# A graph network's first layer: low nodes' counts stored by themselves, dense part begun earlier, fewer edges ahead of it

## The chip, the core and the metric

The kernel runs on one core of a Trainium2 chip. The core has a matrix engine (PE, with its weight loads shown as PEld), a vector engine (DVE), a scalar engine (ACT), a general engine (POOL) and a sequencer that issues most of the transfers (SP). Each engine works through its own instructions in order; engines wait for one another with semaphores. The metric is the device time of one execution in microseconds, smaller is better.

## What is computed

The reference runs four blocks one after the other on 3125 nodes with 256 features and 100000 edges sorted by target node: a two-layer graph attention network, a dense mixture of experts, a two-layer graph convolution, and a routed mixture of experts. The change concerns the first attention layer only:

```python
def gat_conv(x, src, dst, W, a_src, a_dst, bias, concat):
    h = (x @ W).reshape(N, H, C)              # H = 4 heads, C = 256
    al_s = jnp.einsum('nhc,hc->nh', h, a_src)
    al_d = jnp.einsum('nhc,hc->nh', h, a_dst)
    e = jax.nn.leaky_relu(al_s[src] + al_d[dst], 0.2)
    ex = jnp.exp(e - m[dst])                  # m: maximum over the edges of a target
    denom = jax.ops.segment_sum(ex, dst, num_segments=N)
    alpha = ex / denom[dst]
    out = jax.ops.segment_sum(h[src] * alpha[:, :, None], dst, num_segments=N)
```

Each node also has an edge to itself. Targets are drawn so that low node numbers have by far the most edges.

## The kernel before

The class `FirstLayer` does three things in one loop.

*Counts.* The edges are cut into 391 chunks of 256. For each chunk (`count_step`) DVE makes one-hot matrices of the sources' high part (`hot_key`, line 1649) and of their low part (`hot_lo`, on DVE at line 1652 or in three passes on ACT at lines 1655 and 1658), PE multiplies them (line 1666), and the result, a window of 8, 14 or 20 target nodes, goes into an accumulator `acc` of 320 targets: ACT copies all columns but the first (`keep`, line 1683), DVE adds the first (`add`, line 1688). The place in `acc` is a register's value. When all chunks of 320 targets are done (`CUT`, for the first at chunk 128), `piece` opens the next accumulator, `add_own` adds the nodes' own edges and `store_counts` writes 320 columns to DRAM in five transfers. Behind the first of them `low_degrees` (25 matmuls, line 1712) sums the counts of nodes 0 to 255. The later layers need all counts.

*Dense part.* For targets 0 to 255 (`DN`) the layer is computed with dense matrices: the loop reads their counts back from DRAM (`lead`, line 1990), makes the weights on ACT (lines 2003 and 2005) and DVE (line 2010), and PE multiplies them by all source rows (line 2019): 4 heads by 25 blocks of sources, 100 dense steps (`dense_step`).

*Edge part.* For targets from 256 up, 283 chunks of edges are summed one by one (`edge_step`). POOL gathers the source rows, two gathers a chunk, 12 chunks ahead (line 1773); small transfers on SP fetch the targets' terms (`window`, lines 1783 and 1786) two batches of four chunks ahead; PE picks the terms (line 1807) and multiplies (lines 1839 and 1845); DVE adds the result into a sum `agg` of 384 targets (line 1856). For each of the 8 sets of 384 targets, `new_sums` lists tasks: `clear`, then three times `loops` (the nodes' own edges: line 1909 multiplies `x` with the weights `by_node`, which are read back from the DRAM tensor `loops`, spread over all partitions; a transpose and a copy at lines 1914 and 1915 put the weights themselves into the sum), then `done`. `first_terms` writes `loops` at line 1595, one row of 4 numbers per node. Finished sums go through `through_w1` (14 tasks).

The loop in `run` fixes the order by hand. Before it 26 chunks of counts are made, the sums of set 0 are prepared with `new_sums(0)` (a chunk of counts behind each task), and the first batch of edges is prepared. In the loop each step makes one chunk of counts, at most one task from a queue, the edge steps that `share` calls for, and the dense steps that are due. `lead(0)` comes at step `d0` (134), the first dense step four steps later. Up to `d1` = `d0` + 3 the edge steps are spread so that `FIRST` = 45 are done by then; the remaining ones are spread evenly up to the last chunk. After each step PE, DVE and ACT are tied to that order (`in_order`).

## Time and profile before

| | us |
|---|---|
| median of 9 runs | 2705.96 |
| lowest and highest | 2696.09, 2712.39 |
| the profiled execution | 2706.09 |
| its span | 2704.2 |
| first chunk of counts (line 1649) starts | 62.1 |
| last chunk of counts starts | 1119.7 |
| last statistics of the first layer's output (line 1976) | 1164.8 |
| PE, DVE, ACT, POOL busy, share of the span | 87%, 51%, 42%, 30% |

The span begins with the program's first instruction and ends with its last. A line of the profile with a count, such as x782, tells how many instructions it sums; "idle before" is the time for which the engine had nothing to do ahead of them, with what ended it. Matmuls are pipelined, so that the durations of single ones overlap.

### The profile page before, as it was taken

What the parts mean: (1) busy time and instruction counts of PE and PEld (TensorE: products, weight loads), DVE (VectorE), ACT (ScalarE), POOL (GpSimd) and SP (SyncE); (2) the same over time, 40 slices, a digit from 0 to 9 for tenths busy, and PEclk for the clock granted to TensorE, in tenths of its full rate; (3) what the DMA queues carried; (4) which work ended last, traced back from release to release, by engine and by line L of the source; (5) the groups of instructions that cost most, each with busy time, mean ns of one, the idle gap of its engine ahead of it and who ended that gap; (6) DMA issues with size and microseconds to landing.
All of it is one profiled execution on the core that took longest, in us unless ns stands there. A gap on an engine that the chain in (4) does not pass through costs nothing. (4 is left out here: it accounts for less than half of the span.)

```text
span 2704.2 us, 38772 instructions
## 1 busy us (share of the span) xinstructions
PE 2347.1 (87%) x11821; PEld 1905.9 (70%) x11821; DVE 1387.5 (51%) x4378; ACT 1143.5 (42%) x2527; POOL 823.2 (30%) x803
## 2 busy tenths in 40 slices
PE   1488998888888889677999979988989998999997
PEld 1367786766666666466888858877867766888886
DVE  7566546566666677621888844242334664111110
ACT  0256544545555555350444434444433433222221
POOL 1265556656666677120010030000001123122221
PEclk9999868778879888888999979999999998999998
DMA  6543435454554565489512110004324425666662
GB/s 194 83 117 85 116 102 174 112 158 124 167 146 141 168 179 172 122 291 312 171 62 73 62 47 1 1 1 135 121 86 143 135 96 181 190 175 174 190 182 61
DMA packets 242046, 355.01 MB, mean 131 GB/s; under 512 B 45680, under 2 KB 183251, under 8 KB 238114
## 3 DMA queue, kind: packets, MB, share of 16 engines
q1 hardware_dynamic: 198082, 253.10, 30.1%
q0 software_dynamic: 40176, 94.81, 13.9%
q10 hardware_dynamic: 3568, 4.47, 0.5%
q8 instruction: 100, 1.64, 0.3%
q14 instruction: 120, 0.98, 0.1%
HBM read 266.60 MB, written 86.86 MB: 131 GB/s over the span
## 5 line engine op out<-in xcount | busy, mean ns | idle before, releaser
L1773 POOL DMA_INDIRECT edge_rows<-table,pick x566 | 599.3, 1059 | 364.2 <-PE edge_sums L1839 176.7
L1839 PEld LDWEIGHTS edge_sums<-edge_moves,edge_rows 128*128 128x128 f32 x2264 | 380.6, 247 | 60.8 <-DVE agg L1856 20.3
L1839 PE MATMUL edge_sums<-edge_moves,edge_rows 128*128 128x56 f32 (+1 forms) x2264 | 384.5, 328 | 22.8 <-DVE agg L1856 12.0
L1089 PE MATMUL po<-parts,cnt_r 128*128 128x512 f32 x1250 | 329.3, 417 | 14.8 <-ACT cnt_r L1083 14.8
L1089 PEld LDWEIGHTS po<-parts,cnt_r 128*128 128x128 f32 x1250 | 239.9, 197 | 76.8 <-ACT cnt_r L1083 15.6
L1666 PE MATMUL ps<-hot_key,hot_lo 128*128 128x350 f16 (+2 forms) x782 | 229.0, 397 | 71.1 <-DVE agg L1909 16.7
L853 PE MATMUL po<-h,w 128*128 128x257 f32 x1250 | 277.8, 382 | 6.7 <-DVE w L844 4.4
L1683 ACT CAST acc<-ps 128x325 f32 (+2 forms) x391 | 178.5, 457 | 245.0 <-DVE acc L1688 77.7
L853 PEld LDWEIGHTS po<-h,w 128*128 128x128 f32 x1250 | 236.7, 191 | 43.2 <-DVE w L844 6.4
L1649 DVE TENSOR_SCALAR hot_key<-iota_key,key 128x350 f16<-128x350 f16 (+2 forms) x782 | 229.4, 320 | 31.7 <-PE ps L1666 11.1
L2538 ACT ACTIVATE hid<-ph,ffn_b 128x256 f32<-128x256 f32 x232 | 110.0, 474 | 299.5 <-PE ph L2536 298.7
L2536 PE MATMUL ph<-xe,ffn_w 128*128 128x256 f32 x928 | 209.6, 381 | 1.4 <-DVE free L2521 1.4
L2546 PE MATMUL py<-ffn_w,hid 128*128 128x256 f32 x928 | 209.0, 383 | 0.0
L2550 POOL DMA_INDIRECT out<-y,to x58 | 90.4, 1559 | 349.3 <-DVE y L2549 250.0
L2536 PEld LDWEIGHTS ph<-xe,ffn_w 128*128 128x128 f32 x928 | 173.6, 190 | 28.3 <-DVE free L2521 1.6
L2546 PEld LDWEIGHTS py<-ffn_w,hid 128*128 128x128 f32 x928 | 176.1, 192 | 23.2
L1856 DVE TENSOR_TENSOR agg<-agg,edge_sums 128x126 f32 (+1 forms) x283 | 87.2, 308 | 161.4 <-PE edge_sums L1845 70.9
L1655 ACT ACTIVATE hot_lo<-iota_key,lo 128x128 f16<-128x128 f16 x494 | 169.1, 391 | 0.3 <-issue 0.3
L838 ACT ACTIVATE z<-z,att_cols 128x640 f32<-128x640 f32 x125 | 103.0, 828 | 150.4 <-DVE z L836 127.0
L1666 PEld LDWEIGHTS <-hot_lo 128*128 128x128 f16 x782 | 70.4, 114 | 127.1 <-issue 53.4
L2019 PE MATMUL po<-x_rows,w 128*128 128x257 f32 x400 | 148.0, 504 | 1.5 <-issue 1.5
L1083 ACT CAST cnt_r<-cnt_h 128x1920 fp32r<-128x1920 f16 x50 | 89.9, 1799 | 139.6 <-PE po L1089 128.7
(398 smaller groups left out, 3407.4 us busy)
## 6 DMA issues: line engine op xcount, KB each, us to landing
ffn_w<-in_L_ffn_W SPq DMA_DIRECT2D x58, 1024.0 KB
cnt_h<-cnt SPq DMA_DIRECT2D x50, 800.0 KB
rows<-blank SPq DMA_DIRECT2D x109, 258.0 KB
cnt<-acc SPq DMA_DIRECT2D x50, 400.0 KB
cnt<-cnt SPq DMA_DIRECT2D x25, 800.0 KB
normed<-first_out SPq DMA_DIRECT2D x20, 640.0 KB
first_out<-first SPq DMA_DIRECT2D x56, 192.0 KB
edge_rows<-table,pick POOLq DMA_INDIRECT x566
```

The source lines that it names most:

```text
L853: nc.tensor.matmul(pos[i][:, :D + 1], lhsT=w[:, ts(i, P)], rhs=moving[:, j, :D + 1], start=(j == 0), stop=(j == NB - 1))
L1089: nc.tensor.matmul(pos[b], lhsT=c[:, j - j0, ts(b, P)], rhs=parts[i][:, j].rearrange("p a m -> p (a m)"), start=(j == 0), stop=(j == NB - 1))
L1649: nc.vector.tensor_scalar(h[:, u, :NB * w], self.wide[:, :NB * w], self.key[:, t:t + 1], None, op0=ALU.is_equal)
L1655: nc.scalar.activation(l[:, u, :], self.wide[:, :P], AF.Abs, bias=self.lo[:, t:t + 1], scale=-1.0)
L1666: self.nc.tensor.matmul(ps[:, :n], lhsT=l[:, u, :], rhs=h[:, u, :n], start=(u == 0), stop=(u == CT - 1))
L1683: self.nc.scalar.copy(self.acc[g][:, :, ds(o + 1, width(c) - 1)], self.parts[c][:, :, 1:])
L1773: self.nc.gpsimd.indirect_dma_start(out=self.ring[:, e % (RB * BT), :], out_offset=None, in_=self.table, in_offset=bass.IndirectOffsetOnAx ...
L1839: nc.tensor.matmul(ps[:, f * 4 * w:(f + 1) * 4 * w], lhsT=self.rows_of(m)[:, e, ts(f, P)], rhs=self.moves[m][:, e].rearrange("p k w -> p ( ...
L2019: self.nc.tensor.matmul(self.pos[i][:, :D + 1], lhsT=w[:, ts(i, P)], rhs=self.k.rows[:, j, :], start=(j == 0), stop=(j == NB - 1))
L2536: nc.tensor.matmul(ph, lhsT=w1[:, c, ts(f, P)], rhs=xe[:, c, :], start=(c == 0), stop=(c == 1))
L2538: nc.scalar.activation(hid[:, f, :], ph, AF.Gelu, bias=b1[:, f:f + 1])
L2546: nc.tensor.matmul(py, lhsT=hid[:, f, ts(i, P)], rhs=w2[:, f, :], start=(f == 0), stop=(f == NF - 1))
```

## The change

The constant `LOW` is chunk 115, behind which no edge has a target below 256 (`check` has a new test of that, which sends the program to its slow path if the data are otherwise). In the step that keeps chunk 115 the tasks `add_own(0, 0, DN)` and `store_counts(0, 0, DN)` are put at the head of the queue: the counts of nodes 0 to 255 are stored at that point out of the accumulator, which chunks go on filling for nodes 256 to 319; the other 64 columns follow at chunk 128 as before. `low_degrees` goes with the first of these stores. `d0` is 121 and not 134, and `FIRST` is 20 and not 45. Up to chunk 115 `hot_lo` is made on DVE for two chunks of three, where it was one; the rest is on ACT. `loops` in DRAM is turned: four rows, one per head. It is no longer written by `first_terms` but, for each set of 384 nodes, from the transposed weights in `agg`: the transposes become tasks of their own (`turn`), then `store` writes four rows and begins to load, an empty task follows, then the multiplications. `new_sums` so lists 10 tasks for a set of three blocks, not 5, and 31 chunks of counts lie ahead of the loop, not 26.

```diff
@@ -66,6 +66,7 @@
 
 C0 = chunk_of(DN) - 4
 NE = C1 - C0
+LOW = chunk_of(DN) + 3
 NBAT = -(-NE // BC)
 
 CUT = [0] + [chunk_of(GC * g) + 3 for g in range(1, GS)] + [C1]
@@ -73,7 +74,7 @@
 
 WIN = (0, C0, 8), (C0, C0 + 144, 14), (C0 + 144, C1, CW)
 EARLY = 20
-FIRST = 45
+FIRST = 20
 
 
 def width(c):
@@ -1407,7 +1408,7 @@
         self.places = k.dram.tile([NC, CE], F32, name="places")
 
         self.turned = k.dram.tile([P, 2, NP], F32, name="x_turned")
-        self.loops = k.dram.tile([NP - DN, 4], F32, name="loops")
+        self.loops = k.dram.tile([4, NP - DN], F32, name="loops")
         self.inverse = k.dram.tile([AS, 4, GA], F32, name="inverse")
         self.first = k.dram.tile([4, P, 2, NP], F32, name="first_out")
         self.deg_row = k.dram.tile([NB, P], F32, name="deg_row")
@@ -1488,6 +1490,9 @@
                                 ALU.not_equal)
         nc.vector.tensor_scalar(past[:, :C0], row[:, 1, :C0], float(DN), None, op0=ALU.is_ge)
         nc.vector.tensor_reduce(self.k.doubt[:, 0:1], bad, AX.X, ALU.max)
+        nc.vector.tensor_scalar(bad[:, 0:1], row[:, 0, LOW:LOW + 1], float(DN), None,
+                                op0=ALU.is_lt)
+        nc.vector.tensor_tensor(self.k.doubt[:, 0:1], self.k.doubt[:, 0:1], bad[:, 0:1], ALU.max)
 
     def load_edges(self, src_cols, dst_cols, pool):
         nc = self.nc
@@ -1592,7 +1597,6 @@
         nc.vector.tensor_add(own, st[:, DB:, :n], t[:, DB:, :])
         nc.vector.scalar_tensor_tensor(own, own, 0.0, st[:, DB:, n:], op0=ALU.max, op1=ALU.add)
         nc.scalar.activation(own, own, AF.Exp, scale=0.8)
-        nc.sync.dma_start(self.loops.rearrange("(b p) k -> p b k", p=P), own)
         nc.vector.memset(self.own[:, :, n:], 1.0)
 
         gap = pool.tile([1, 2, n], F32, name="gap1")
@@ -1640,6 +1644,11 @@
         if g:
             nc.vector.tensor_copy(acc[:, :, :EXT], self.acc[g - 1][:, :, GC:])
 
+    def by_vector(self, c):
+
+
+        return c < EARLY or (c % 3 == 0) == (c > LOW)
+
     def make(self, c):
         nc, w = self.nc, width(c)
         h = self.hot.tile([P, CT, NB * CW], F16, name="hot_key")
@@ -1648,13 +1657,13 @@
             t = c * CT + u
             nc.vector.tensor_scalar(h[:, u, :NB * w], self.wide[:, :NB * w], self.key[:, t:t + 1],
                                     None, op0=ALU.is_equal)
-            if c < EARLY or c % 3 == 0:
+            if self.by_vector(c):
                 nc.vector.tensor_scalar(l[:, u, :], self.wide[:, :P], self.lo[:, t:t + 1], None,
                                         op0=ALU.is_equal)
             else:
                 nc.scalar.activation(l[:, u, :], self.wide[:, :P], AF.Abs,
                                      bias=self.lo[:, t:t + 1], scale=-1.0)
-        if not (c < EARLY or c % 3 == 0):
+        if not self.by_vector(c):
             nc.scalar.activation(l, l, AF.Relu, bias=1.0, scale=-1.0)
         self.hots[c] = h, l
 
@@ -1678,8 +1687,8 @@
         g, o = self.place_of(c)
         if c == CUT[g] and g:
             self.piece(g)
-            self.tasks.appendleft(lambda: self.store_counts(g - 1))
-            self.tasks.appendleft(lambda: self.add_own(g - 1))
+            self.tasks.appendleft(lambda: self.store_counts(g - 1, DN if g == 1 else 0, GC))
+            self.tasks.appendleft(lambda: self.add_own(g - 1, DN if g == 1 else 0, GC))
         self.nc.scalar.copy(self.acc[g][:, :, ds(o + 1, width(c) - 1)], self.parts[c][:, :, 1:])
 
     def add(self, c):
@@ -1687,22 +1696,22 @@
         col = self.acc[g][:, :, ds(o, 1)]
         self.nc.vector.tensor_tensor(col, col, self.parts.pop(c)[:, :, 0:1], ALU.add)
 
-    def add_own(self, g):
+    def add_own(self, g, n0, n1):
 
         acc = self.acc[g]
         for j in range(NB):
-            a, e = max(j * P, g * GC), min((j + 1) * P, (g + 1) * GC)
+            a, e = max(j * P, g * GC + n0), min((j + 1) * P, g * GC + n1)
             if a < e:
                 own = acc[:, j, a - g * GC:e - g * GC]
                 self.nc.vector.tensor_add(own, own, self.ident[:, a - j * P:e - j * P])
 
-    def store_counts(self, g):
+    def store_counts(self, g, n0, n1):
         n = g * GC // GW
         o = g * GC - n * GW
         for j in range(0, NB, 5):
-            self.nc.sync.dma_start(self.k.cnt[n, :, j:j + 5, o:o + GC],
-                                   self.acc[g][:, j:j + 5, :GC])
-        if g == 0:
+            self.nc.sync.dma_start(self.k.cnt[n, :, j:j + 5, o + n0:o + n1],
+                                   self.acc[g][:, j:j + 5, n0:n1])
+        if n0 == g == 0:
             self.low_degrees()
 
     def low_degrees(self):
@@ -1724,9 +1733,12 @@
             self.add(i - 3)
         if 2 <= i <= C1 + 1:
             self.keep(i - 2)
+        if i - 2 == LOW:
+            self.tasks.appendleft(lambda: self.store_counts(0, 0, DN))
+            self.tasks.appendleft(lambda: self.add_own(0, 0, DN))
         if i == C1 + 2:
-            self.tasks.append(lambda: self.add_own(GS - 1))
-            self.tasks.append(lambda: self.store_counts(GS - 1))
+            self.tasks.append(lambda: self.add_own(GS - 1, 0, GC))
+            self.tasks.append(lambda: self.store_counts(GS - 1, 0, GC))
 
 
 
@@ -1887,21 +1899,31 @@
             a = self.agg[q] = self.work.tile([P, 9, GA + EXT], F32, name="agg1", bufs=2)
             self.nc.vector.memset(a[:, :, n:], 0.0)
             self.nc.vector.memset(a[:, 8, :n], 0.0)
-            load(0)
 
         st = {}
+
+        def turn(i):
+            pt = self.aux.tile([P, 512], F32, name="aux")
+            self.nc.tensor.transpose(pt[:5, :P], self.own[:, blocks[i] - DB, :], self.k.ident)
+            self.nc.scalar.copy(self.agg[q][:5, 8, ts(i, P)], pt[:5, :P])
 
         def load(i):
             b = blocks[i]
             x = self.work.tile([P, 2, P], F32, name="loop_x", bufs=2)
             self.nc.sync.dma_start(x, self.turned[:, :, ts(b, P)])
             w = self.work.tile([P, 4 * P], F32, name="by_node", bufs=3)
-            self.nc.sync.dma_start(w, self.loops[(b - DB) * P:(b - DB + 1) * P, :].rearrange(
-                "n k -> (n k)")[None, :].to_broadcast([P, 4 * P]))
+            self.nc.sync.dma_start(w.rearrange("p (k n) -> p k n", k=4),
+                                   self.loops[:, (b - DB) * P:(b - DB + 1) * P][None].to_broadcast(
+                                       [P, 4, P]))
             st[i] = x, w
 
+        def store():
+            o = (blocks[0] - DB) * P
+            self.nc.sync.dma_start(self.loops[:, o:o + n], self.agg[q][:4, 8, :n])
+            load(0)
+
         def loops(i):
-            nc, a, k = self.nc, self.agg[q], self.k
+            nc, a = self.nc, self.agg[q]
             x, w = st.pop(i)
             if i + 1 < len(blocks):
                 load(i + 1)
@@ -1909,15 +1931,14 @@
             nc.vector.tensor_tensor(
                 a[:, :8, ts(i, P)].rearrange("p (c k) n -> p c k n", c=2),
                 x[:, :, None, :].to_broadcast(shape),
-                w.rearrange("p (n k) -> p k n", k=4)[:, None].to_broadcast(shape), ALU.mult)
-            pt = self.aux.tile([P, 512], F32, name="aux")
-            nc.tensor.transpose(pt[:5, :P], self.own[:, blocks[i] - DB, :], k.ident)
-            nc.scalar.copy(a[:5, 8, ts(i, P)], pt[:5, :P])
+                w.rearrange("p (k n) -> p k n", k=4)[:, None].to_broadcast(shape), ALU.mult)
 
         def done():
             self.ready = q
 
-        return [clear] + [lambda i=i: loops(i) for i in range(len(blocks))] + [done]
+        each = range(len(blocks))
+        return ([clear] + [lambda i=i: turn(i) for i in each] + [store, lambda: None]
+                + [lambda i=i: loops(i) for i in each] + [done])
 
     def turn_over(self, q):
 
@@ -2141,7 +2162,7 @@
             self.spread_edges(0)
             self.open_dense()
             e = s = 0
-            i0, d0 = i, CUT[1] + 6
+            i0, d0 = i, LOW + 6
             engines, last = [mybir.EngineType.PE, mybir.EngineType.DVE, mybir.EngineType.Activation], {}
             start = len(nc.cur_bb.bb.instructions)
```

## The prediction

> **What bounds the kernel now.** The profiled execution took 2706.09 us (span 2704.2), the median of nine runs is 2705.96, so every sum below is made against 2706.1. I read the page's slices first (each 67.6 us), then the stretches of the first layer, then its time order, to find which wait ends last in each.
>
> ```profile
> PE   1488998888888889677999979988989998999997
> DVE  7566546566666677621888844242334664111110
> ```
>
> The edit touches slices 2 to 17 alone; all behind them (from 1165 us on) is the same program. Next the layer cut at its own borders, by the starts of the counts' L1649 (two per chunk of counts): chunk 26, the loop's first, starts at 135.8 us, chunk 31 at 151.3, chunk 124 at 284.4, chunk 138 (the first with a dense step) at 311.7, the last chunk, 390, at 1119.7. Columns: length, busy us of PE, PE's weight loads, DVE, ACT and POOL, granted clock, DMA share, GB/s.
>
> ```profile
> 110.00:152.00 42.00, 12.72 (x63) 8.04 (x63) 23.37 (x68) 11.85 (x42) 31.16 (x27) 1.00 0.83 152
> 152.00:284.00 132.00, 118.79 (x667) 98.67 (x666) 85.39 (x424) 90.20 (x287) 72.79 (x76) 1.00 0.35 91
> 312.00:1120.00 808.00, 703.54 (x4255) 545.36 (x4254) 517.58 (x1735) 425.73 (x1108) 494.98 (x478) 0.82 0.52 146
> ```
>
> PE is busy 30% of the start-up, 90% of the short stretch (counts and few edges) and 87% of the long one. Line L1666 (two per chunk) and L1839 (eight per edge step) alone, in the last two stretches, PE busy first:
>
> ```profile
> 152.00:284.00 132.00, 44.65 (x185) 17.87 (x184) 1.00 0.35 91
> 312.00:1120.00 808.00, 159.94 (x506) 42.64 (x506) 0.82 0.52 146
> ...
> 152.00:284.00 132.00, 68.75 (x298) 68.09 (x298) 1.00 0.35 91
> 312.00:1120.00 808.00, 301.99 (x1902) 298.60 (x1901) 0.82 0.52 146
> ```
>
> So the short stretch holds 92 chunks and 37.2 edge steps, the long one 253 chunks, 238 edge steps, 100 dense steps. Prices on PE: in the short stretch 44.65/92 = 0.49 us a chunk, and (118.79-44.65)/37.2 = 1.99 us an edge step; in the long one 159.94/253 = 0.63 and, with L1845 (62.57) and L1807 (38.26), 402.8/238 = 1.69. An edge step is dearer in the short stretch, though it is narrower there. The time order says why:
>
> ```profile
> 201.01 1.93 PE L1839 MATMUL edge_sums<-edge_moves,edge_rows 128*128 128x56 f32 x8
> ...
> 299.50 5.24 PE L1712 MATMUL aux<-acc,ones_h 128*128 128x256 f16 x25 [2.36 <-DVE acc L1697]
> ...
> 305.17 0.99 PE L1839 MATMUL edge_sums<-edge_moves,edge_rows 128*128 128x56 f32 x8
> ```
>
> The same eight matmuls take 1.93 us before the 25 back-to-back ones of `low_degrees` and 0.99 us right after them: whatever the clock column prints (1.00), PE runs at half speed up to 304 us. In the long stretch the clock is 0.82.
>
> Start-up, in order of time:
>
> ```profile
> 104.02 1.79 SPq L1595 DMA_DIRECT2D loops<-own_w  x1
> ...
> 121.82 0.34 SPq L1899 DMA_DIRECT2D by_node<-loops  x1
> ...
> 126.00 1.99 DVE L1909 TENSOR_TENSOR agg<-loop_x,by_node 128x1024 f32<-128x1024 f32 x1 [14.49 <-DMA by_node<-loops]
> ...
> 128.31 0.49 PE L1666 MATMUL ps<-hot_key,hot_lo 128*128 128x200 f16 x2 [16.75 <-DVE agg L1909]
> ```
>
> A store of 2944 pieces of 16 bytes takes 17.8 us until the load that waits for it is issued; behind that load DVE stands 14.5 us, and with it PE and ACT.
>
> **The change, part by part.**
>
> *1. `loops` stored turned (4 rows), `turn` ahead of `loops`.* The 16-byte store goes; four rows of 1.5 KB replace it. On SP the new store stands behind two window loads, which wait for the other 16-byte store (`terms`, complete at 116.1 us now). Then 1.5 us of issues (four at 0.38), the store, and a load: the same load took 3.7 us from issue to completion; for the store no row of this size exists, bounds 1 and 4 us, I take 2. The first multiplication starts at 116.1+1.5+0.3+2+3.7 = 123.6 us; were `terms` complete at 112.2, its first piece, 119.7. I take 122 (126.0 before). In DVE's program order 27 chunks are then made instead of 21.5: the wait is filled. From there to the loop: 3 multiplications at 1.22 us (part 2) and 4 chunks at about 1 us = 8 us. Loop begins at **130 us with 31 chunks done** (bounds 127.5 and 134), against 135.8 with 26.
>
> *2. The multiplication reads `by_node` in runs.* L1909 takes 1.99 us with stride-4 reads; L1958, same shape and contiguous, 1.22. 23 of them: 0.77 x 20 = 15.4 us of DVE in the loop. DVE is busy 64% of the long stretch, so I count a third: **-5 us** (bounds 0 and -15). The `turn` tasks are the same transposes and copies in their own steps. The queue of one task a step grows by 5 entries per set of 384 nodes (24 entries where 26 to 47 steps lie between sets), and two more entries are left behind the last chunk: products there take about 1.5 us: **+2 us** (bounds 0 and 4).
>
> *3. Short stretch with 20 edges, not 45.* From chunk 31 to 118, where `LOW` acts: 87 chunks, 18.7 edges. PE at half speed: 87 x 0.49 + 18.7 x 1.99 = 80 us. `by_vector` gives two of three chunks' `hot_lo` to DVE instead of one. ACT: (42.16+25.82)/62 = 1.10 us a chunk saved on 29 chunks; its need is 87 x 0.35 + 29 x 1.10 = 62 us. DVE: a chunk made wholly on DVE has a period of 0.79 us (starts of L1688 from 96.77 to 99.14, 0.79 apart); the 85.39 us less 37.2 edges at 0.69 leave 0.65 a chunk now, so one with ACT's help is 0.58; after, 0.72 x 87 + 18.7 x 0.69 + 3 x 1.22 = 79 us. Without this edit ACT would need 94 us: it is the cover of the stretch. Two engines at 80 us in lock step: at 85% (PE has 90% alone) 94 us, and 5 us to fill the edges' chain. Chunk 118 starts at 130+99 = **229 us** (bounds 88 and 112 for the 99).
>
> *4. Counts of nodes 0 to 255 stored at chunk 118, dense part from 125, not 138.* New wait: these five stores read `acc`, which the following chunks go on writing; in program order ACT's next L1692 copy waits for all five, and so does DVE's next add. Now five stores are issued in 6.1 us at 293.97, into a buffer that nobody writes on. Behind ACT's copy are the `hot_lo` passes, behind DVE's add all `hot_key`: everything stops. Price 6.1 + 2 = 8 us, within which `low_degrees` (5.24 on PE, moved here from chunk 131) runs; bounds 5 and 12. On SP the stores and the two `cnt` loads that wait for them stand ahead of `window` loads, which are needed two batches, 8 edge steps, later: nothing. Seven chunks at 1.07 and this: 125 starts at 229+15.5 = **244.5 us**. The later border at chunk 128 keeps its 3.39 us memset (L1639), now inside the long stretch: +4.
>
> *5. Long stretch.* It had 808 us; now 13 chunks and 25 edges more, all dense steps as before. Lower bound by PE's prices: 13 x 0.63 + 25 x 1.69 = 50 us; upper bound by length over edges, 808/238 = 3.39 each: 85 us. PE's idle share kept, /0.87: 9.5 + 25 x 1.94 = **58 us**. I take it because PE is the busiest engine. The last chunk starts at 244.5+808+58+4-5 = 1109.5 us and the tail gives 2 back: 1111.5 against 1119.7, **-8 us: 2698**.
>
> The Trainium skill speaks against part 3: "TensorE: Matmul & The Clock Gate", "The HAM clock gate", lets the clock rise after one busy window of about 3.4 us. This trace does not agree: 90% busy from 152 to 284 us, and still 1.9 us for eight matmuls. If it rose there, an edge step would cost about half, and taking 25 out would save some 20 us less: about 2718 by the rule, an estimate.
>
> **Rivals.**
> *Slower: the edge steps set the long stretch.* One mechanism: each edge step needs two row gathers on POOL, in order:
>
> ```profile
> L1773 POOL DMA_INDIRECT edge_rows<-table,pick x566 | 599.3, 1059 | 364.2 <-PE edge_sums L1839 176.7 <-issue 99.1 <-PE edge_sums L1845 34.6
> ```
>
> 2 x (1.059+0.30) = 2.72 us an edge, 80% of its 3.39 us share. Leave out the edges and the sum is 1063 us; 57 us are left for 25 edges, so from **2.28 us an edge** the change loses. At 2.72: +11, 2717; at 3.39: 2734. Against it: POOL waits mostly for PE's release of a ring place. 20%.
> *No change.* Edge price near 2.2, or start-up still held to 126 us and the stall at 118 worth 12: 2706. 12%.
> *More gained.* The 25 edges fall into PE's 104 idle us of the long stretch at 1.2 each, part 2 counts whole: 1111.5 - 18 - 10 = 1083.5, so 2670 us. For it: DVE and ACT have room. Against: PE's idle lies inside chains. 18%.
> *It doesn't do what it says:* the turned store waits as long as the old one; 4 us, inside my range.
>
> **How the numbers follow.** Forecast 2698 (own range 2686 to 2706), 50%. A measurement of this kernel tells 0.2% (5.4 us) from no change. Below 2700.7 lie 35 of the forecast's 50, so: forecast 35 faster and 15 same, more gained 18 faster, no change 12, edge-bound 20 slower: faster 0.53, same 0.27, slower 0.20. Range 2672 to 2718: to "more gained" below and the gathers' 2.72 us above.
>
> **What would show it.** Right: first L1931 near 122 us at 1.22 us; chunk 118 near 229; a stop of 5 to 12 us on ACT's L1692 behind L1712's stores; first dense multiplication near 247; the last chunk near 1110; L1839 at about 0.23 us each before chunk 118. Wrong: the short stretch over 110 us (DVE the new bound), a long stretch over 890 us, or a clock there that leaves 0.80 to 0.84, since 25 edges more change how dense PE's work is.

## The result, and the profile after

The changed kernel is slower: 2761.02 us in the median of ten runs (2750.2 to 2778.53), against 2704.85 us of the kernel before on the same chip, a ratio of 1.0204 (95% interval 1.0181 to 1.0226). Ratios and their intervals go by the runs within 1.5% of a kernel's fastest, medians by all its runs. The forecast was 2698. The profiled execution took 2764.16 us, its span is 2762.4.

All of it lies in the first layer. From the end of its last `bn_stats` to the end of the span, the two traces take 1539.4 and 1539.5 us. Ahead of that, by the starts of the same chunks:

| stage | before | forecast | after |
|---|---|---|---|
| start of chunk 31 | 151.3 | 130 | 143.5 |
| chunks 31 to 118 | 124.9 | 99 | 109.5 |
| 118 to the dense part's first step | 35.5 | 15.5 | 15.9 |
| long stretch, to the start of chunk 390 | 808.0 | 865 | 894.2 |
| tail, to the last `bn_stats` | 45.1 | 47 | 59.8 |

The page's slices of the changed kernel, each 69.1 us:

```profile
PE   2468999998899888869799979997998998999997
DVE  7567545555666656631588872433334664111111
```

PE stands at 80% or more in the 4th to the 17th slice (3rd to 16th before). The stretches of the changed kernel (columns as before: length, busy us of PE, weight loads, DVE, ACT, POOL, granted clock as a share of full speed, DMA share, GB/s):

```profile
110.00:143.50 33.50, 7.25 (x30) 3.08 (x30) 14.07 (x62) 7.98 (x27) 25.56 (x24) 1.00 0.55 138
143.50:253.00 109.50, 80.93 (x425) 60.04 (x426) 84.55 (x428) 58.41 (x185) 36.59 (x38) 1.00 0.26 69
...
269.00:1163.00 894.00, 806.22 (x4600) 637.24 (x4599) 532.66 (x1837) 441.74 (x1152) 536.29 (x527) 0.75 0.50 140
1163.00:1223.00 60.00, 37.64 (x74) 17.27 (x73) 17.30 (x37) 9.21 (x20) 0.00 (x0) 0.60 0.28 93
```

and the end of the kernel before, for the last row:

```profile
1120.00:1165.00 45.00, 25.25 (x66) 12.48 (x66) 15.60 (x34) 8.63 (x19) 0.00 (x0) 0.85 0.33 107
```

PE's 80.93 and DVE's 84.55 us in the short stretch are near the 80 and 79 us of the forecast, yet it took 109.5 and not 99. In the long stretch PE is busy 90% (87% before) at a clock of 0.75 (0.82 before). The tail has the same work at 0.60 instead of 0.85. The counts' multiplications (L1675) and the edge steps' eight (L1851) by stretch, PE busy first:

```profile
143.00:253.00 110.00, 41.53 (x174) 17.91 (x174) 1.00 0.26 69
269.00:1163.00 894.00, 182.22 (x530) 44.91 (x530) 0.75 0.50 140
...
143.00:253.00 110.00, 35.35 (x152) 34.84 (x152) 1.00 0.26 69
269.00:1163.00 894.00, 367.74 (x2103) 368.47 (x2102) 0.75 0.50 140
```

In the long stretch a chunk costs PE 182.22/266 = 0.69 us (0.63 before), the eight multiplications of an edge step 367.74/263 = 1.40 (1.27 before): both are dearer.

The start-up and the stop at chunk 118, from the time order:

```profile
117.20 0.02 SPq L1922 DMA_DIRECT2D loops<-agg  x1
...
124.40 2.82 SPq L1915 DMA_DIRECT2D by_node<-loops  x3
...
126.47 1.22 DVE L1931 TENSOR_TENSOR agg<-loop_x,by_node 128x1024 f32<-128x1024 f32 x1 [8.82 <-DMA by_node<-loops]
...
135.54 1.23 DVE L1931 TENSOR_TENSOR agg<-loop_x,by_node 128x1024 f32<-128x1024 f32 x1 [4.66 <-DMA loop_x<-x_turned]
```

```profile
261.65 0.26 DVE L1697 TENSOR_TENSOR acc<-acc,ps 128x25 f32 x1 [7.45 <-DMA cnt<-acc]
```

The multiplication takes 1.22 us as forecast, but starts at 126.5 and not 122, and the third one waits 4.66 us more, for its `x`. The stop behind the five stores is there: 7.45 us (8 forecast).

### The profile page after: what moved, and what is told of

The parts are those of the page before. It is cut to its first block, busy times and chain, and to the rows that moved or that the text cites. A ratio compares the mean times of both kernels' runs of the same rounds, so it can differ in the third digit from the quotient of the medians.

```text
span 2762.4 us, 38775 instructions
## 1 busy us (share of the span) xinstructions
PE 2406.3 (87%) x11821; PEld 1948.0 (71%) x11821; DVE 1380.4 (50%) x4444; ACT 1116.7 (40%) x2431; POOL 809.5 (29%) x803
## 3 DMA queue, kind: packets, MB, share of 16 engines
q0 software_dynamic: 40176, 94.81, 13.5%
q8 instruction: 100, 1.64, 0.2%
## 5 line engine op out<-in xcount | busy, mean ns | idle before, releaser
L1785 POOL DMA_INDIRECT edge_rows<-table,pick x566 | 586.1, 1036 | 418.1 <-PE edge_sums L1851 224.7
L1851 PEld LDWEIGHTS edge_sums<-edge_moves,edge_rows 128*128 128x128 f32 x2264 | 405.1, 260 | 73.9 <-issue 24.5
L1851 PE MATMUL edge_sums<-edge_moves,edge_rows 128*128 128x56 f32 (+1 forms) x2264 | 404.9, 340 | 29.7 <-DVE agg L1868 13.2
L1675 PE MATMUL ps<-hot_key,hot_lo 128*128 128x350 f16 (+2 forms) x782 | 244.9, 415 | 73.8 <-DVE acc L1697 26.6
L1675 PEld LDWEIGHTS <-hot_lo 128*128 128x128 f16 x782 | 71.7, 115 | 133.6 <-issue 55.5
L839 ACT ACTIVATE z<-z,att_cols 128x640 f32<-128x640 f32 x125 | 103.0, 828 | 150.5 <-DVE z L837 127.6
L2040 PE MATMUL po<-x_rows,w 128*128 128x257 f32 x400 | 160.2, 539 | 0.9 <-issue 0.9
L1664 ACT ACTIVATE hot_lo<-iota_key,lo 128x128 f16<-128x128 f16 x430 | 147.2, 390 | 0.6 <-issue 0.6
```

Source lines behind the costliest of these rows:

```text
L1664: nc.scalar.activation(l[:, u, :], self.wide[:, :P], AF.Abs, bias=self.lo[:, t:t + 1], scale=-1.0)
L1675: self.nc.tensor.matmul(ps[:, :n], lhsT=l[:, u, :], rhs=h[:, u, :n], start=(u == 0), stop=(u == CT - 1))
L1785: self.nc.gpsimd.indirect_dma_start(out=self.ring[:, e % (RB * BT), :], out_offset=None, in_=self.table, in_offset=bass.IndirectOffsetOnAx ...
L1851: nc.tensor.matmul(ps[:, f * 4 * w:(f + 1) * 4 * w], lhsT=self.rows_of(m)[:, e, ts(f, P)], rhs=self.moves[m][:, e].rearrange("p k w -> p ( ...
L2040: self.nc.tensor.matmul(self.pos[i][:, :D + 1], lhsT=w[:, ts(i, P)], rhs=self.k.rows[:, j, :], start=(j == 0), stop=(j == NB - 1))
```

## The experiments

The kernels of a group ran on one chip beside the kernel before, so ratios within a group compare like with like. The result above counts as group 1. Absolute times of different groups do not compare, and that became a finding: the kernel before took 2690 to 2705 us in groups 1, 2 and 6 ("slow groups" below), 2590 to 2593 us in groups 3, 4 and 5 ("quick groups"). The expectations put this down to the chip. That is not shown: the record gives groups 5 and 6 the same chip number, 10. Groups 1 and 2 are 15 us apart in the median of the kernel before, so a difference between stages of these two groups is good to some 15 us, or 0.6 us for each of 25 edge steps.

### Group 2, a slow group: the parts by themselves

**The share alone.** In the kernel before:

```diff
-FIRST = 45
+FIRST = 20
```

> The kernel before with one edit: 20 instead of 45 edge steps ahead of the dense part. The work is the same; 25 edge steps move from the short stretch into the long one. Theory A, an edge step of the long stretch has a fixed price of about 3.4 us (808 us / 238 before, 894 / 263 after), against 1.99 us of PE in the short stretch: +25 x (3.39 - 1.99) = +35 us, ratio about 1.013, long stretch (chunk 138 to 390) about 263 x 3.39 = 892 us whatever the granted clock. Theory B, the granted clock falls with the mix (0.82 before, 0.75 after): the long stretch gets about as long, and its clock falls towards 0.75. Theory C, the loss came from the start-up, the turned store and the store at chunk 118 and not from the share: within 5 us of before. The prediction's 1.94 us an edge: 0 us.

Ratio 1.0126 (1.0074 to 1.0178), +34 us. The sum is theory A's, its terms are not. Stretches of this kernel, from chunk 31, 118, 138 and 390:

```profile
147.40:249.50 102.10, 75.32 (x381) 50.52 (x382) 70.92 (x357) 82.51 (x265) 31.85 (x34) 1.00 0.21 54
249.50:282.70 33.20, 23.79 (x113) 13.78 (x112) 21.78 (x87) 22.26 (x65) 6.75 (x7) 1.00 0.40 117
282.70:1138.40 855.70, 751.59 (x4567) 588.04 (x4566) 531.52 (x1789) 426.74 (x1114) 542.88 (x527) 0.81 0.52 146
```

Against the profile of before in group 1, the long stretch grew by 47.7 us for 25 edge steps, 1.91 each: near the forecast's price, not 3.39. Its clock stayed at 0.81 (0.82 before), so the fall that theory B asks for did not come, and the loss came without it. What is missing is the other side. Chunks 31 to 138 became only 25.1 us shorter (135.3 against 160.4), 1.0 us for each edge step taken out, although PE lost more than 40 us there: ACT, 82.51 us of 102, had become the busiest engine. The tail is 11 us longer.

**The share back.** In the changed kernel, `FIRST = 45`.

> The changed kernel with 45 edge steps ahead of the dense part again; turned loops, early store, early dense part stay. Theory A: the long stretch has 238 edge steps again, 238 x 3.4 = 809 us in place of 894, the short one 25 x 2.0 to 2.4 us = 50 to 60 us more: -25 to -35 us against the changed kernel, ratio to before 1.007 to 1.011. Theory B: as much, and the long stretch's clock comes back to about 0.82; if it stays near 0.75 with 238 x 3.4 us, A holds and B does not. Theory C: 2755 to 2765 us, ratio 1.02.

Ratio 1.0068 (1.004 to 1.0095): 1.4% below the changed kernel's. Its long stretch took 822.6 us (forecast for this share: 808 + 9.5 + 4 - 5 = 816.5), at a clock of 0.80:

```profile
308.00:1131.00 823.00, 726.14 (x4286) 562.65 (x4284) 519.53 (x1785) 439.87 (x1148) 485.88 (x478) 0.80 0.51 144
```

Against the changed kernel's profile in group 1, the last 25 edge steps cost 894.2 - 822.6 = 71.6 us, 2.86 each, and saved 34.6 us between chunks 31 and 125, 1.4 each.

**The dense part's start put back.** In the changed kernel:

```diff
-            i0, d0 = i, LOW + 6
+            i0, d0 = i, CUT[1] + 6
```

> The changed kernel with the dense part's start back at the chunk where it was (138 in place of 125); 20 edge steps ahead, early store and turned loops stay. Theory A: the long stretch is 263 edge steps x 3.4 us wherever it begins, and the 13 chunks ahead of it cost 13 x 1.1 us: +14 us against the changed kernel, ratio to before about 1.025. Theory B: the same dense work beside 13 chunks fewer is a denser mix; clock nearer 0.82 and the long stretch under 870 us: ratio 1.01 to 1.015. Theory C (the early start itself costs): the kernel comes back towards before, ratio 1.00 to 1.01.

Ratio 1.0214 (1.0166 to 1.0262), from four runs. Against the 1.0204 of group 1, beginning the dense part 13 chunks sooner is worth nothing that can be measured, either way. Theory B's and theory C's ratios are out; so are the 892 us of theory A's long stretch, which took 847.7.

**The turned loops alone** in the kernel before: the new `loops`, `turn`, `store` and L1931, nothing else.

> The kernel before with only the turned store of loops, the turn steps and the contiguous multiplication. Theory A and B: chunk 31 starts about 8 us sooner as in the changed kernel (143.5 against 151.3), the long stretch keeps its 238 edge steps and about 808 us: -5 to -8 us, ratio about 0.997. Theory C: the load of by_node through DRAM within the loop (7.9 us of waits of DVE in the long stretch after) and the start-up cost 10 us or more: ratio 1.004 or higher.

Ratio 1.0052 (1.0028 to 1.0076). The part that the forecast counted as a gain of 5 us and an earlier start lost some 14 us here. Group 6 comes back to it.

### Group 3, a quick group: price or clock

**The kernel before again**, unchanged.

> The kernel before, unchanged, on the chip of this group: ratio 1.000 within 0.3%. Its profile says how far two profiles of one kernel lie apart stage by stage; every theory needs that the long stretch (808 us), the tail (45 us) and the rest of the program (1539 us) come again within about 10 us. If the tail is 55 to 60 us here, as in the four kernels tried so far, the 15 us of the tail are no effect of the change.

Ratio 0.9994 (0.9962 to 1.0026), but at 2592.82 us. Stretches of this profile of the kernel before (from chunk 31, 118, 138, 390):

```profile
149.00:261.00 112.00, 108.96 (x629) 94.24 (x628) 80.22 (x398) 83.97 (x270) 70.03 (x74) 1.00 0.40 105
...
296.00:1005.00 709.00, 655.72 (x4256) 515.78 (x4255) 517.14 (x1732) 423.65 (x1109) 501.96 (x478) 0.87 0.59 166
1005.00:1060.00 55.00, 34.65 (x66) 15.99 (x66) 16.27 (x36) 8.61 (x19) 0.00 (x0) 0.63 0.27 89
```

The rest of the program takes 1539.9 us again. The long stretch takes 709.5 us in place of 808: an edge step's "price" of 3.39 us is 2.98 here, so it was no constant, and theory A falls. The tail takes 54.3 us at a clock of 0.63 in the unchanged kernel: the 15 us of the tail above are the clock's chance, seen at 45 and at 54 in one kernel. Of the 98 us, PE is busy for 48 less, at a clock of 0.87 in place of 0.82, and idle for 51 less. Some of the idle time shows in the waits of the long stretch. The first fence is the profile of before, the second this one (us in total, times, longest):

```profile
PEld L1666 <- issue: 23.6, 51, 3.7
PEld edge_sums L1839 <- issue: 16.3, 24, 2.5
PEld aux L1807 <- issue: 13.0, 8, 5.0
...
ACT first L1973 <- remote: 17.7, 5, 5.1
```

```profile
PEld L1666 <- issue: 8.1, 28, 0.6
PEld edge_sums L1839 <- issue: 2.2, 8, 0.3
...
PEld aux L1807 <- issue: 0.5, 2, 0.3
```

In the first, PE, its weight loads and ACT stand for 39.7 + 79.6 + 32.2 = 151 us in waits that the profile puts down to nothing (`issue`), up to 5 us long; in the second for 17 us, none over 1. These are sums over three engines whose waits overlap; the `remote` line is not in them.

**More work for PE.** In the changed kernel, with a tile `none` of zeros, behind each multiplication of a dense step:

```diff
+            for _ in range(4 if j < NB - 1 else 0):
+                self.nc.tensor.matmul(self.pos[i][:, :D], lhsT=self.none,
+                                      rhs=self.wide[:, :D], start=False, stop=False)
```

> The changed kernel with eight more f16 multiplications of 256 columns, by a tile of zeros, in each dense step (they add nothing to the sums; 792 in all, 0.105 us each at full clock by low_degrees' 0.21 us at half, so 83 us of PE at full clock). Theory P, an edge step has a fixed price of 3.4 us: PE has 88 us idle in the long stretch, its length grows by 0 to 25 us, ratio to before 1.02 to 1.03. Theory W, the length is PE's work at full clock (busy us times granted clock, 605 us now) over the granted clock and PE's busy share of 0.90: if the clock stays at 0.75, (605+83)/0.75/0.90 = 1019, +125 us, ratio 1.066; if the denser work lifts the clock to 0.90, 849 us, -45 us, ratio 1.004. In both cases busy us of PE times clock over length stays near 0.68 to 0.72 under W only if the clock stays.

2628.87 us, ratio 1.0129 (1.0074 to 1.0184), with a clock of 0.94 in the long stretch. PE's busy time by the clock there is 688 us, 87 above the changed kernel's 601: the work was added and was as large as reckoned. At a clock held at 0.75 the expectation had 125 us for it.

**Dense steps two by two**, in the changed kernel with a third `w`:

```diff
-                        s * (C1 - 12 - d0) <= (i - d0 - 3) * len(self.steps):
+                        (s | 1) * (C1 - 12 - d0) <= (i - d0 - 3) * len(self.steps):
```

> The changed kernel with the dense steps issued two by two (a third buffer for w), same work. Theory P: no change, ratio 1.018 to 1.023. Theory W: the same PE work in another order, the length follows the granted clock: if pairs lift it from 0.75 to 0.82 the long stretch falls to 605/0.82/0.90 = 820 us, ratio 0.993; if the clock stays, no change.

Ratio 1.0077 (1.0046 to 1.0107), 2609.77 us; the long stretch took 764.8 us at 0.86. This reads only against the changed kernel in a quick group, which the next one has: 1.0065 there, so issuing the dense steps in pairs changed nothing that can be measured.

**More edge steps early**, `FIRST = 65` in the kernel before.

> The kernel before with 65 in place of 45 edge steps ahead of the dense part. Theory P: 20 x (3.39 - 2.2) = 24 us less, ratio 0.991. Theory W: 20 edge steps at 1.0 us of full-clock work are 20/0.82/0.88 = 28 us less in the long stretch, against 20 x 1.99/0.9 = 44 us more in the short one at half clock: +16 us, ratio 1.006. The prediction's prices (1.94 and 1.99): 0 to +5 us.

Ratio 0.9971 (0.994 to 1.0003). Against the profile of before in this group, the long stretch lost 709.5 - 668.6 = 40.9 us for 20 edge steps (2.05 each) and chunks 31 to 138 grew by 180.0 - 147.2 = 32.8 (1.64 each). Both prices were close to the forecast's 1.94 and 1.99; the gain is the difference, and hardly measurable.

### Group 4, a quick group: the changed kernel again

**The changed kernel**, unchanged.

> The changed kernel, unchanged, on the chip of this group. The kernel before took 2690 to 2705 us on the chips of the first two groups and 2590 on that of the third, with the difference in the long stretch alone (808 against 709.5 us). Theory S (shares and prices): the ratio is 1.015 to 1.022 on any chip, since the moved edge steps are dearer in the long stretch by about 1 us each. Theory K (the chip's stalls): most of the loss is waits that the profile can't put down to anything (PE, its weight loads and ACT together 143 us in the long stretch of the changed kernel, 19 to 25 us in the third group); on a chip without them the ratio falls to 1.005 or below, on one with them it stays at 1.02.

2631.25 us in the median of ten runs, 1.0147 times before's 2593.1; the ratio, from five of the ten, is 1.0065 (1.0011 to 1.0119). The ten run from 2592 to 2659 us, where the 31 runs of the kernel before keep within 41 us. Most stand in step with the mean granted clock: 0.921 and 0.922 for the runs at 2615 to 2618, 0.911 for 2627 and 2635, 0.897 to 0.902 for 2655 to 2659. Two runs, 2592 at 0.896 and 2648 at 0.866, fall out of the order; there is no profile of these two. Its long stretch, 257 to 1034 us, and the time order at the second set of the nodes' own edges:

```profile
257.00:1034.00 777.00, 715.72 (x4603) 568.90 (x4602) 529.05 (x1838) 438.30 (x1153) 539.12 (x527) 0.84 0.57 161
```

```profile
148.91 1.22 DVE L1931 TENSOR_TENSOR agg<-loop_x,by_node 128x1024 f32<-128x1024 f32 x1 [8.15 <-DMA by_node<-loops]
```

Here the first L1931 starts at 122.9 and chunk 31 at 130.6 us: the forecast's 122 and 130. All turned kernels in quick groups begin chunk 31 between 127.6 and 131.7 us, in slow groups between 136 and 148. Against the profile of before in group 3 (medians 2590 there and 2593 here), the stages are 18.0 us shorter up to chunk 31, 3.3 shorter from 31 to 118, 17.8 shorter up to the dense part, 67.7 longer in the long stretch and 3.8 in the tail. So here the start came as forecast, and the short stretch missed its forecast gain of 26 us by more than the long one missed its 57.

**Half of the added work** (`range(2 ...)` in the edit above).

> The changed kernel with four more f16 multiplications of 256 columns by zeros in each dense step (half of the earlier run's, 42 us of PE at full clock). Theory W with the clock lifted by denser work: within 10 us of the changed kernel or faster than it. If PE's work sets the length at an unchanged clock: 42/0.80/0.9 = 58 us slower than the changed kernel, ratio to before about 1.04. If PE does not set it: 0 to 5 us.

Ratio 1.0058 (1.0024 to 1.0092), 2611.8 us in the median, all ten runs in 2599 to 2632. The changed kernel has 2631 in this group and a ratio of 1.0065: with 42 us more work on PE the kernel is 19 us faster by the medians of ten runs and the same by the ratios, and its profile's long stretch is 14 us shorter. So the work cost nothing, where an unchanged clock asked for 58 us:

```profile
256.40:1019.70 763.30, 705.78 (x4984) 552.84 (x4984) 527.06 (x1838) 437.45 (x1153) 538.49 (x527) 0.92 0.58 164
```

PE has 381 multiplications more and is busy 10 us less; the eight multiplications of the edge steps take it 292 us in all, in place of 325. The clock went from 0.84 to 0.92.

**The changed kernel with 65 edge steps early**, `FIRST = 65`.

> The changed kernel with 65 in place of 20 edge steps ahead of the dense part. By what the first runs showed (an edge step 1.0 to 1.6 us in the short stretch, 1.9 to 2.9 in the long one): 45 x (1.0 to 1.3) = 45 to 58 us faster than the changed kernel, ratio to before 0.999 to 1.004. By the prediction's prices (1.99 and 1.94): as fast as the changed kernel, 1.02. If the short stretch is full of PE work from 45 on (90% busy before): near the kernel with 45, ratio 1.007.

Ratio 1.0027 (0.9996 to 1.0057): with 65 edge steps early the changed kernel is within noise of before. Its long stretch:

```profile
316.70:1020.00 703.30, 633.48 (x4025) 487.93 (x4023) 506.29 (x1739) 433.57 (x1141) 449.10 (x439) 0.87 0.56 159
```

Against the changed kernel of this group it lost 777.2 - 703.3 = 73.9 us for 45 edge steps, 1.64 each, and chunks 31 to 125 grew by 60.7, 1.35 each. The direction is again that of the share.

**The turned loops alone**, as in group 2.

> The kernel before with the turned loops alone, a second time, on another chip. It cost 0.5% (0.3 to 0.8) in the second group although its profile's first layer ended no later than before's. If that was the chip: ratio 0.993 to 1.000, from a loop that starts 8 to 18 us sooner. If the extra trip of by_node through DRAM within the loop costs it: 1.003 to 1.008 again.

Ratio 0.9956 (0.9913 to 0.9999), 2587.16 us: a small gain here, a small loss in group 2. Its chunk 31 starts 17.5 us sooner than in the profile of before in group 3, but chunk 118 only 5 us sooner (256.2 against 261.1): between chunks 35 and 40 it takes 15.6 us, before 6.3.

### Group 5, a quick group: the clock held up

**The turned loops alone, with work added**: four multiplications by zeros in each dense step.

> The kernel before with the turned loops and with four zero-weight f16 multiplications in each dense step (42 us of PE at full clock, nothing added to the sums). Theory W (the long stretch is PE's work over the granted clock; denser work lifts the clock from 0.83 to 0.87 up to 0.92): long stretch (566+42)/0.92/0.92 = 718 us against 709 on a chip like that of the last group, so 0 to +10 us against the turned loops alone, ratio 0.995 to 1.000 there; the gain is in the kernel whose clock is low, the changed one. If the added work only costs: +50 us, ratio 1.015.

Ratio 0.9986 (0.9947 to 1.0024), as expected: the added work neither cost nor gained. The clock is 0.94, against 0.86 without the work in group 4:

```profile
289.00:991.50 702.50, 649.14 (x4637) 506.18 (x4636) 500.06 (x1734) 423.72 (x1108) 490.72 (x478) 0.94 0.59 168
```

**Both stretches of the changed kernel**: the same four in each dense step and, for chunks 31 to 124, in `multiply`:

```diff
+            for _ in range(4 if u == 0 and 30 < c < 125 else 0):
+                self.nc.tensor.matmul(ps[:, :n], lhsT=self.none, rhs=self.wide[:, :n],
+                                      start=False, stop=False)
```

> The changed kernel with zero-weight f16 multiplications in both stretches: four of 200 columns in each chunk of counts from 31 to 124, four of 256 in each dense step. Theory W: the eight matmuls of an edge step fall from about 1.9 to 1.0 us in the short stretch once the clock rises there, its 109 us become about 90 (DVE's 83 us over 0.92), against the 42-us variant of the last group another -15 to -20 us, ratio to before 0.998 to 1.002. If the clock does not rise in the short stretch, its PE work grows by 87 x 0.7 = 61 us to 140 us: +40 us, ratio 1.02.

Ratio 1.0065 (1.0031 to 1.01). The clock rose in the short stretch, from 161 us on: the eight multiplications of an edge step, 1.84 us in the changed kernel of group 4, took 1.02 here (L1856 is L1851, moved down by the edit):

```profile
200.79 1.02 PE L1856 MATMUL edge_sums<-edge_moves,edge_rows 128*128 128x56 f32 x8
```

Chunks 31 to 118 took 108.3 us all the same (109.2 there), and from chunk 40 on, most of it at the raised clock, 86 us as there. So neither line of the expectation came true for that stretch: with 20 edge steps PE does not set it. In the long stretch this kernel and the one before it in this group, with clocks of 0.93 and 0.94, differ by 756.2 - 702.6 = 53.6 us, for 25 edge steps and 13 chunks. The forecast had 48.5 + 9.5 = 58.

```profile
259.00:1015.00 756.00, 693.89 (x4986) 545.40 (x4985) 528.78 (x1838) 437.43 (x1152) 543.01 (x527) 0.93 0.58 165
```

**The same for the turned loops alone**, with two multiplications a chunk up to chunk 137, and 45 (first) or 65 edge steps early.

> The kernel before with the turned loops and zero-weight multiplications in both stretches: two of 200 columns in each chunk from 31 to 137, four of 256 in each dense step. If the clock rises in the short stretch: PE's 111 us there become 65 to 70, ACT's 84 us set it, 95 to 100 us in place of 125, ratio 0.985 to 0.990. If it stays at half: 87 x 0.35 = 30 us more, ratio 1.005 to 1.01.

> As h3_turned_kept_warm with 65 in place of 45 edge steps ahead of the dense part. If the short stretch runs at full clock an edge step costs 1.0 us there and 2.0 to 2.9 in the long one: 20 to 35 us less than h3, ratio 0.975 to 0.982. If it stays at half clock: 20 x (1.6 to 2.2) more there, 20 x 2.0 to 2.9 less in the long stretch: as h3 within 10 us.

Ratios 0.9975 (0.9942 to 1.0008) and 1.0041 (1.001 to 1.0072). Two multiplications a chunk lifted the clock only here and there in the short stretch of the first (for 7 us from 175, 24 from 202 and 37 from 246 on, the eight at about 1.0 us there and at 1.84 elsewhere), and in that of the second not before 299 us (1.84 up to there). So a short stretch at full clock with 65 edge steps was not reached.

### Group 6, a slow group: the wait behind the new store

**The changed kernel with a distance behind the store**, sets 1 to 7:

```diff
-        return ([clear] + [lambda i=i: turn(i) for i in each] + [store, lambda: None]
+        return ([clear] + [lambda i=i: turn(i) for i in each] + [store] + [lambda: None] * (9 if q else 1)
                 + [lambda i=i: loops(i) for i in each] + [done])
```

> The changed kernel with nine empty steps in place of one between the store of a set's turned loops and its first multiplication (sets 1 to 7; set 0, ahead of the loop, as it was). In the fourth group's profile of the changed kernel DVE waited 8.1 us for by_node at the second set (chunks 35 to 40 took 16.4 us, the five after them 5.0) and 11.4 us at later sets. Theory D (one step of some 1.2 us does not cover a store and a load through DRAM): chunks 35 to 40 in about 6 us, chunk 118 about 9 us sooner (231 in place of 240 on a chip like that one), long stretch up to 11 us shorter: -9 to -20 us against the changed kernel, ratio to before 1.005 to 1.011. If that wait was covered anyway (DVE would have waited for PE a moment later): less than 3 us.

Ratio 1.0173 (1.0137 to 1.0209), against 1.0204 without it in group 1: about 8 us, with intervals that overlap. The stretch itself is clear, although this profile is that of the fastest of the six runs (2719.7 us, median 2739.7). Chunks 35 to 40 took 4.8 us (17.0 in the changed kernel), and 31 to 118 took 100.3. The stretch, and the first multiplication of the second set from the time order:

```profile
146.00:246.00 100.00, 80.95 (x424) 59.91 (x425) 83.95 (x426) 58.16 (x184) 37.18 (x38) 0.50 0.28 74
```

```profile
163.49 1.22 DVE L1931 TENSOR_TENSOR agg<-loop_x,by_node 128x1024 f32<-128x1024 f32 x1
```

The first row has the same work as the changed kernel's in 9 us less. (Its clock column shows 0.50, the other's 1.00, at the same busy time of PE: the one trace holds a record of half clock there, the other holds none.) The second is the multiplication that had waited 8 us, now without a wait.

**The same in the turned loops alone.**

> The same edit in the kernel before with the turned loops (counts, dense part and 45 edge steps as before). There DVE waited 7.2 us at the second set and 19.1 us at five later ones. Theory D: -7 to -26 us against the turned loops alone (0.9956 on one chip, 1.0052 on another), so 0.986 to 0.993 on a chip like the fourth group's. If the wait was covered anyway: 0.994 to 0.997. The most this kernel can win over before is the start (18 us) and the multiplications (15 us): 0.987.

Ratio 0.9993 (0.9967 to 1.0018), against 1.0052 (1.0028 to 1.0076) of the turned loops in group 2. So the loss went with the wait, though this is read across two groups; and even without the wait nothing is won in a slow group.

No version was shown to beat the kernel before in both kinds of group; the turned loops alone (0.9956) and 65 edge steps early (0.9971) came nearest, in quick ones.

## Why the prediction was wrong, point by point

The forecast for the first layer was -8 us, the profiles have +58. Of the 66 us between, 29 lie in the long stretch, 13.5 in the start, 13 in the tail and 10.5 in the short stretch.

**The long stretch (part 5)** is the step that failed most there: 57 us forecast, 86 measured. Its term "25 edges at 1.94 us" was built from PE's prices and its idle share at a clock of 0.82, both taken as fixed. Where the clock was about the same in two kernels it came out near: 1.91 us with the share alone (0.81), 2.05 with 65 edge steps early in group 3 (0.87 and 0.90), and 53.6 us against 58 for the term with the 13 chunks in group 5 (0.93 and 0.94). In the changed kernel the clock fell to 0.75 (0.84 in group 4, where before has 0.87 in group 3), and PE's work, 601 us by busy time and clock (575 before), took 806. At before's clock and busy share these 601 us would make a stretch of 601/0.817/0.871 = 845 us, 37 more than before's; by this estimate the other 49 of the 86 go with the fall of the clock, less what PE's smaller idle share gave back. The same estimate for the quick groups gives 38 and 30 us of 68. The 2.86 us for each of the 25 edge steps is read across two groups; within group 4 the price was 1.64. The forecast named "a clock there that leaves 0.80 to 0.84" as what would break it, and gave that no price.

That the clock acts on PE's work is shown by the half of the added work in group 4: at 0.92 in place of 0.84 PE did 42 us more work in less busy time. That the low clock also sets the length is argued and not shown: no run raised the clock clearly without adding work (the dense steps two by two had 0.86 and no gain), and the gain of 19 us by the medians is not in the ratios. What turns the clock down in this mix is not settled. The turned loops add waits of DVE, and the changed kernel without them had 0.78 and 870 us in the slow group 6, in its fastest run; but the turned kernels with 45 edge steps had 0.80 to 0.83 in slow groups with or without such waits.

The move of the edge steps loses even with the clock where it was: the share alone, at 0.81, cost 34 us. The 25 edge steps saved only 1.0 us each ahead of the dense part there, with ACT the busiest engine, and 1.4 in the changed kernel, less than the 1.94 that the forecast itself had for them in the long stretch.

The rival with 3.39 us an edge step gave 2734 for about this price. It was right in direction and wrong in mechanism: gathers and edge steps are no fixed price, as before's own 2.98 in a quick group shows.

**The short stretch (part 3)** gained 15 us in place of 26, and 3 in the quick groups, where before itself took 112.5 us for it and not 124.9. Its estimate of two engines in lock step was good: 100.3 us once the wait was out (group 6), 99 forecast. What it lacked is the wait behind the new store, 8.8 us for `by_node` at the second set:

```profile
162.28 1.23 DVE L1931 TENSOR_TENSOR agg<-loop_x,by_node 128x1024 f32<-128x1024 f32 x1 [8.81 <-DMA by_node<-loops]
```

Part 2 had counted the `turn` tasks as "the same transposes and copies in their own steps". It did not ask what the store between them makes wait: the store and the load that reads it back lie one step of about 1.2 us ahead of the multiplication. DVE stood ready at 153.5 us; SP, behind window loads, issued the store at 157.3 and the load at 158.9, and its data was there at 162.3. Part 1 priced this very trip, 2 + 3.7 us, for the first set alone.

**The start (part 1)** was forecast at 130 us and is 128 to 132 us in quick groups, 143.5 in the profile of group 1. The order of the waits was right. What was off is a duration in that group: from the store to the load SP took 7.2 us there, with the loads between them 1.4 to 2.2 us apart, and 2.3 us in group 4, with the same loads 0.6 us apart or less. That makes the first multiplication 4.5 us late. Of the other 9 us, the third multiplication's wait for `x` has 4.66 (0.2 in group 4) and a wait of DVE for `edge_turn` 3.9, both for loads on SP again.

**The early store (part 4)**: 7.45 us for 8, chunks 118 to 125 in 15.9 us for 15.5. Right.

**The earlier dense part** was treated as free to move, and is, within the noise, as the start put back shows.

**The multiplication (part 2)**: 1.22 us, right in its duration; the -5 us drawn from it can be seen in no run, while DVE's waits in the same tasks took 8.8 us at the second set and 7.9 at later ones.

**The tail**: 47 forecast, 59.8 measured, at a clock of 0.60. The unchanged kernel had 45 and 54 us, so for all but some 5 us the forecast lacked a width here and not a mechanism.

**The clock's rise.** The Trainium skill's page cited, "TensorE: Matmul & The Clock Gate", "The HAM clock gate", lets the clock rise after one busy window. The runs do not agree with that for every kind of work: 90% busy with these multiplications of 56 columns, and 97% in group 3 (108.96 of 112 us), did not lift the clock; four more of 200 columns a chunk did. The 20 us that the prediction hung on a rise were for 45 edge steps at full clock, which no run had for the whole stretch; with 20 edge steps the rise gained nothing, because PE does not set that stretch then.

## What to carry to other kernels

A price per step that was read at one granted clock holds only if the mix leaves the clock alone; when work is moved into a stretch where PE is the bound, say what the time would be at the next lower clock too. Taking work out of a stretch pays only down to its next engine: read the two columns behind the busiest one before counting a saving in full. A store that is read back through DRAM needs a distance in steps (here 5.0 us from its issue to the data, against one step of 1.2), and every set that repeats it needs the distance, not the first alone.

## What the runs showed that had not been expected

One program takes 2590 or 2700 us, by the group in which it ran: the difference is in the first layer's loop alone. In the long stretch about half of it is PE's longer busy time at a lower clock (48 us), and half its idle time, with waits of up to 5 us without a named cause (151 us summed over PE, its weight loads and ACT, against 17). What these waits are, and whether the chip makes the difference, was not tried. A change in the gathers' time is not the reason: 1061 and 1076 ns each.

More work can cost nothing: 42 us of multiplications by zeros did not make the changed kernel slower, at a clock of 0.92 in place of 0.84.

The mean granted clock of a run can be read only with its records: with the turned loops alone in group 2 one run of 2702.4 us showed 0.865 and another of 2702.3 us 0.910. The profile of the former holds a record of half clock over 263 us from 48 us on, which by itself takes 0.049 off its mean, over a stretch for which other profiles hold no record at the same speed.
